# Two record tiles loaded apart, dropped nodes stored ahead of the other keys, merged loads and batch-norm statistics in a graph-layer kernel

## The chip, the core and the metric

The kernel runs on one core of a Trainium2 chip. The metric is the device time of one launch in microseconds (us), the median of several executions. The profile is one more execution, recorded by the hardware profiler. Engines: TensorE (PE), VectorE (DVE), ScalarE (ACT), GpSimd (POOL) and SyncE (SP). SP issues the plain transfers, POOL the indirect ones (gathers and scatters by a list of rows).

## What is computed

Sixteen batches of 1024 nodes with 64 channels, and for each batch a 1024 x 1024 adjacency with positive weights (about 4 neighbours in 1024 on average, but up to some 90 for the first nodes, whose probability is highest).

```python
# layer 0
h = maximum(layernorm(x), 0)
x = x + (adj / clip(sum(adj, 2), 1)) @ h
# layer 1
h = maximum(layernorm(x), 0)
nb   = (adj > 0) without the diagonal;  m = nb.sum(-1);  rank = cumsum(nb)
skip = (m + 1) // 2 where m > 10 (and the node is not masked)
removed = nb & (rank % skip == 0);  rem = removed | removed.T
valid = nb & ~rem, and the node itself
agg  = 0.25 * q25 + 0.5 * q50 + 0.25 * q75    # quantiles of h over the valid neighbours, per channel
x = x + (relu((h + agg) @ W1 + b1) @ W2 + b2) * mask
```

A node with more than ten neighbours drops two of them, and these must also drop it.

## The kernel before

`list_path` (lines 386 to 1485) does all the work; `dense_path` is a fallback behind a flag that stays zero with these inputs.

**A planner writes the order.** `Plan` (lines 246 to 345) runs when the program is built. Every stage is a Python generator that yields the engine of its next step and the earliest time it is thought to be ready; the planner emits, step by step, the stage that can begin first, and breaks ties by rank. The costs are those of `Plan.note` (a POOL indirect transfer takes 1.27 us and lands 2.2 us later, and so on). DVE and POOL keep exactly this order; the order of the others is settled by the framework's scheduler. Each engine executes its list in order, so an instruction that waits holds up all behind it, and a wrong guess of the planner becomes a wait.

**First stage, per batch** (`loads`, `beginnings`, `signs`, `listing`, `transposes`, `products`, `channels`, `endings`, lines 574 to 823). Eight tiles of 128 rows of the adjacency arrive, 512 KB each, in tiles named `at`. ACT takes signs (`sg`) with the row's sum; DVE multiplies them by position keys and takes the eight largest keys of each of four segments (`rec`): a record of up to 32 neighbours. PE transposes `at` (`pt`), ACT copies the result (`att`), PE multiplies (`ps_small`), DVE divides by the degree and adds x. `normed` (line 518) is the layer norm, called twice in each batch (for x, and for the sum): DVE sums, ACT squares with an accumulated sum in eight pairs of instructions (`ln_sq`), DVE and ACT make the root, ACT scales. The result and the record make up a row of 164 numbers (`row`). `endings` ranks the nodes by number of neighbours and scatters the rows, eight POOL calls in each batch, into a sorted table `srt`; the channels go to a table `tab`.

**Second stage, per group of four batches** (`group`, lines 1187 to 1322; four groups). When the 32 scatters of a group have landed, all 32 record tiles are loaded (`recs`, 544 KB, line 1202), the node numbers computed (`nodes_i`), and the adjacency rows of the 128 nodes with most neighbours gathered (`gat_rows`, line 1216). DVE counts and checks the lists (`gfound`, `gm`, `over`), searches the keys of 31 tiles (lines 1244 to 1253), removes dropped neighbours, and only then counts along the gathered rows (lines 1278 to 1291) which two columns each of these nodes drops. Two POOL calls store the dropped numbers in `tab` (`tab<-drop,didx`, lines 1293 to 1303). After these have landed, a `Job` for each of eleven list lengths gathers the neighbours' channels from `tab` (`places`, one POOL call for each neighbour place and tile, 124 in a group), sorts them by a network of DVE minima and maxima, weighs them, runs the two small layers and scatters the result (`out_dram`, 31 calls in a group). A job also loads its own channels (`S`, line 874) and its residual (`y`, line 1131), each with a transfer of its own.

**Third stage, the long lists** (`long_lists`, lines 1324 to 1458): the nodes with most neighbours of all batches, 128 at a time, in four lists of up to 88, 28, 21 and 18 neighbours. The order of adding the stages is:

```python
for g in range(NG - 1): plan.add(group(g), -2000)
...
with tc.tile_pool(name="long", bufs=1) as pool:
    plan.add(group(NG - 1, pool, "last_"), -2000)
    plan.add(long_lists(pool), -1500)
```

The last group and the long lists begin when the first stage has given back its memory.

Of the kernel before, what the change touches and what calls it, by code (L numbers as in the profile page):

```python
# [9 lines left out]
F32 = mybir.dt.float32  # L10
# [8 lines left out]
P = 128  # L19
# [366 lines left out]
def list_path(ctx, tc, x, adj, nodemask, w1, b1, w2, b2, out, go):  # L386
# [97 lines left out]

    before = consts.tile([P, NT], F32, name="before")
# [32 lines left out]
    def normed(h, xt):  # L518

        s = new(tiny, [P, NT], F32, "ln_s", 4)  # L520
        nc.vector.tensor_reduce(s, xt, AX.X, OP.add)
        nc.vector.tensor_scalar(s, s, -1.0 / C, None, op0=OP.mult)
        v = new(tiny, [P, NT], F32, "ln_v", 4)
        for t in range(NT):
            if t % 2 == 0:
                yield "ACT", lambda: at(s)
            sq = new(tiny, [P, C], F32, "ln_sq", 2)
            nc.scalar.activation(
                sq, xt[:, t, :], AF.Square, bias=s[:, t:t + 1], accum_out=v[:, t:t + 1]
            )  # L530
        yield "DVE", lambda: at(v) + SLACK
# [42 lines left out]
    def loads(pool, now):  # L574
        def nodes(st, b):
            yield "SP", lambda: room("xt", 3)
            st["xt"] = new(pool, [P, NT, C], F32, "xt", 3, users=1)
            nc.sync.dma_start(st["xt"], x[b].rearrange("(t p) c -> p t c", p=P))
            st["mrow"] = new(tiny, [NT, P], U8, "mrow", 3)
            nc.sync.dma_start(st["mrow"], nodemask[b].rearrange("(t p) -> t p", p=P))  # L580

        yield from nodes(batch[0], 0)
        for b, st in enumerate(batch):
            now[0] = b
            for t in range(NT):
                if t == 2 and b + 1 < B:
                    yield from nodes(batch[b + 1], b + 1)
                yield "SP", lambda: room("at", 5)
                st["rows"][t] = new(pool, [P, N], F32, "at", 5, users=2)
                nc.sync.dma_start(st["rows"][t], adj[b, t * P:(t + 1) * P, :])  # L590

    def beginnings(pool, now):

        for b, st in enumerate(batch):
            now[0] = b
            yield "DVE", lambda: max(known(st, "xt", "mrow"), room("h0", 3), room("row", 4))
            mrow_f = new(tiny, [NT, P], F32, "mrow_f", 2)
            nc.vector.tensor_copy(mrow_f, st["mrow"])

            h0 = new(pool, [P, NT, C + 1], F32, "h0", 3, users=2)  # L600
# [3 lines left out]
            yield from normed(h0[:, :, :C], st["xt"])  # L604
            st["h0"] = h0
            yield "PE", lambda: max(at(mrow_f), room("ps_small", 3))
            pm = new(ps_s, [P, HALF], F32, "ps_small", 3, users=1)
            nc.tensor.transpose(pm[:, :NT], mrow_f, ident[:NT, :NT])
            yield "ACT", lambda: at(pm)
            nc.scalar.copy(row[:, :, RW - 1], pm[:, :NT])  # L610
            nc.scalar.copy(row[:, :, RW - 2], row_f)
            free(pm)

    def signs(pool, now):
        for b, st in enumerate(batch):
            now[0] = b
            for t in range(NT):
                yield "ACT", lambda: max(
                    at(st["rows"][t]) if t in st["rows"] else INF, room("sg", 4),
# [4 lines left out]
                sg = new(pool, [P, N], HF, "sg", 4, users=1)  # L624
# [112 lines left out]
    def channels(pool, now):  # L737

        for b, st in enumerate(batch):
# [3 lines left out]
            yield from normed(row()[:, :, :C], row()[:, :, X1:R0])  # L743
# [100 lines left out]

    class Job:
# [3 lines left out]
        def __init__(self, pool, n, T, keys, idx, node, mask, nodes_i, table, S, g, name="places",  # L849
                     bufs=4, rank=0, half=False, begin=0.0):  # L850
# [6 lines left out]
        def run(self):  # L857
# [6 lines left out]
                self.begin, at(self.idx), room(self.name, self.bufs), room("S", 4) if short else 0.0  # L864
# [6 lines left out]
            if short:  # L871
                mine = self.S
                self.S = new(pool, [P, T, C], F32, "S", 4, users=1)
                nc.sync.dma_start(self.S, mine[:, :, :C])
                self.residual = mine[:, :, X1:R0]
# [248 lines left out]
        def layers(self, terms, sources):  # L1124

            T, R = self.T, terms[0][0].shape[1]
            yield "PE", lambda: max(at(*sources) + LOOSE, room("y", 6), room("pt", 2))
            y = new(mlp, [P, T, CO], F32, "y", 6, users=1)
            x1 = y
            if self.short:  # L1130
                nc.sync.dma_start(x1, self.residual)
            else:
                x1 = self.S[:, :, X1:R0]
# [52 lines left out]

    def group(g, kept=grp, name=""):

        size = GROUPS[g]
        four = size == 4  # L1190
        caps, caps_sb, s = (CAPS, caps4, 0) if four else (CAPS2, caps2, 2)
        NTAU = len(caps)
        begin = 1 if four else 0
        R = FIRST[g] + size

        yield "SP", lambda: 0.0 if progress["batches"] >= R and (
            g < 2 or name or progress["jobs"][g - 2] == len(set(CAPS[1:] if GROUPS[g - 2] == 4 else CAPS2))
        ) else INF
        table = tabs[g]
        recs = new(kept, [P, NTAU, REC], F32, name + "recs", 1 if name else 2)  # L1200
        tiles = srt[g].rearrange("(t p) w -> p t w", p=P)
        nc.sync.dma_start(recs, tiles[:, :, R0:])
        yield "DVE", lambda: at(recs)
        lists = recs[:, :, :8 * NSEG]
        node = recs[:, :, REC - 2]
        mask = recs[:, :, REC - 1]
        nodes = new(grp, [P, NTAU], F32, "nodes", 1)
        nc.vector.tensor_scalar(
            nodes, node, noff[:, s:s + 1], float(FIRST[g] * N), op0=OP.add, op1=OP.add
        )  # L1210
        nodes_i = new(kept, [P, NTAU], I32, name + "nodes_i", 1 if name else 2)
        nc.vector.tensor_copy(nodes_i, nodes)
        progress["begun"] = g + 1
        yield "POOL", lambda: at(nodes_i)
        full = new(grp, [P, N], F32, "gat_rows", 1)
        gather(full, adj_rows, nodes_i[:, 0:1])
        yield "DVE", always

        found = new(grp, [P, N], BF, "gfound", 1)[:, :NTAU * 8 * NSEG]
        found = found.rearrange("p (t e) -> p t e", t=NTAU)  # L1220
        nc.vector.tensor_scalar(found, lists, 0.0, None, op0=OP.is_gt)
        m = tiny.tile([P, NTAU], F32, name="gm")
        nc.vector.tensor_reduce(m, found, AX.X, OP.add)
        over = tiny.tile([P, NTAU], F32, name="over")
        nc.vector.tensor_reduce(
            over, found.rearrange("p t (s e) -> p t s e", e=8)[:, :, :, 7], AX.X, OP.max
        )
        nc.vector.memset(over[0 if four else HP:, 0:1], 0.0)
        big = tiny.tile([P, NTAU], F32, name="big")
        nc.vector.tensor_tensor(big, m, caps_sb, OP.is_gt)  # L1230
        nc.vector.tensor_tensor(over, over, big, OP.max)
        nc.vector.tensor_reduce(ovf[:, g:g + 1], over, AX.X, OP.max)

        base = toff[:, s:s + 1]
# [4 lines left out]

        drop = new(tiny, [P, 2, 2], F32, "drop", 2)  # L1240
# [3 lines left out]
        for t in range(begin, NTAU):  # L1244
            nc.vector.max(out=keys[:, t, :8], in_=lists[:, t, :])
            if caps[t] > 8:
                nc.vector.match_replace(
                    out=left, in_to_replace=keys[:, t, :8], in_values=lists[:, t, :],
                    imm_value=0.0,
                )  # L1250
                nc.vector.max(out=keys[:, t, 8:], in_=left)
            if t % 8 == 0:
                yield "DVE", always

        assert all(cap <= T_THRESH for cap in caps[begin + 1:])
        fst = slice(begin, begin + 1)
        skip = dilation(m[:, fst], mask[:, fst], 1)
# [6 lines left out]
        if four:  # L1264
# [504 lines left out]
```

## Time and profile before

| | |
|---|---|
| median of three executions | 1457.18 us (1456.25 to 1458.25) |
| the profiled execution | 1457.89 us |
| its span, first to last instruction | 1456.0 us |
| DVE busy | 1214.5 us |
| POOL busy | 960.6 us |
| PE busy | 745.0 us |
| ACT busy | 579.9 us |
| scatters of batches 0, 1, 2, 3 begin | 67.8, 100.6, 136.0, 168.6 us |
| first gather of `places` | 213.3 us |
| last scatter of batch 15 begins | 885.6 us |
| last gather of `places` ends | 1383 us |

How to read it. All recorded instructions carry line 240, that of a helper, so a group is known by its tiles: `places<-tab,idx` writes `places` from `tab` by the list `idx`. A view of waits says for which engine's instruction the engine sat idle, and for how long in all, how often, and at most. "issue" is idle time with no releaser in the profile: the gap between two POOL calls that follow one another is of this kind. A view of stages gives the busy time of each engine within a stretch of the span.

### The profile page before, as it was taken

The page shows a single profiled execution, that of the slowest core. Times are in us where ns is not written, and L with a number is a line of the kernel's source. Part 1 is how long each engine was busy: PE and PEld are TensorE (multiplying, and loading weights), DVE is VectorE, ACT ScalarE, POOL GpSimd, SP SyncE. Part 2 cuts the span into 40 slices and gives each one's busy share as a digit, 9 for nine tenths or more (in the row PEclk, how much of TensorE's full clock was granted, in tenths as well). Part 3 has the DMA queues.
Part 4 walks back from the last instruction along what each step waited for, and adds up shares of the span by engine and source line. Part 5 has one row for each costly group of instructions (what it writes and reads, how often), then busy time and mean ns, then how long its engine had stood idle before and what let it go on. Part 6 is the DMA issues. An engine that isn't in the chain of part 4 may idle for free.

```text
span 1456.0 us, 14752 instructions
## 1 busy us (share of the span) xinstructions
PE 745.0 (51%) x3186; PEld 463.6 (32%) x3186; DVE 1214.5 (83%) x4039; ACT 579.9 (40%) x1747; POOL 960.6 (66%) x1120
## 2 busy tenths in 40 slices
PE   4777877345697566783666660002300262134674
PEld 2434434223345434352443430001200141134453
DVE  6868798997989968899766874868999979999885
ACT  7989978444656527672353830000000010001110
POOL 0132227777767887677778576577777877777754
PEclk9879998668697687895587775555555575558576
DMA  5445567524464416472232334121111111212100
GB/s 183 138 128 184 176 199 203 137 52 143 100 175 117 107 34 181 121 191 78 71 108 76 87 70 89 42 55 44 37 23 24 27 29 27 41 34 46 24 16 14
DMA packets 134589, 132.20 MB, mean 91 GB/s; under 512 B 100196, under 2 KB 102884, under 8 KB 134372
## 3 DMA queue, kind: packets, MB, share of 16 engines
q1 hardware_dynamic: 102972, 91.00, 21.8%
q0 software_dynamic: 31520, 40.19, 12.8%
q8 instruction: 27, 0.44, 0.1%
q14 instruction: 70, 0.57, 0.1%
HBM read 111.62 MB, written 23.61 MB: 93 GB/s over the span
## 4 chain that ended last, share of the span: by engine, by line
DVE 36%; POOL 22%; issue 11%; PE 10%; DMA 10%; ACT 9%; SPq 0%; DVEq 0%; POOLq 0%; ACTq 0%
POOL places L240 14%; DVE places L240 6%; PE ps_small L240 5%; PE pt L240 5%; DMA at<-in_adj_dram 5%; DVE lplaces L240 4%; DVE other L240 4%; DVE rec L240 4%; DMA places<-tab,idx 3%; POOL out_dram L240 3%; ACT sg L240 3%; DVE l0other L240 3%; POOL lplaces L240 2%; ACT ln_sq L240 2%; DVE sg L240 2%
## 5 line engine op out<-in xcount | busy, mean ns | idle before, releaser
L240 POOL DMA_INDIRECT places<-tab,idx x372 | 375.5, 1009 | 114.5 <-issue 106.7
L240 PE MATMUL pt<-ident,prod 128*128 128x128 f32 (+1 forms) x736 | 162.0, 383 | 389.8 <-DVE prod L240 325.0
L240 PE MATMUL ps_small<-att,h 128*65 128x512 f32 x512 | 254.3, 644 | 27.9 <-ACT att L240 9.4
L240 PEld LDWEIGHTS pt<-ident,prod 128*128 128x128 f32 (+1 forms) x736 | 131.6, 264 | 422.2 <-issue 250.6
L240 POOL DMA_INDIRECT srt<-row,to x128 | 130.3, 1018 | 179.4 <-ACT row L240 158.6
L240 PE MATMUL pt<-ident,at 128*128 128x128 f32 x1024 | 168.4, 309 | 65.9 <-ACT att L240 51.8
L240 DVE MAX8 rec<-sg 128x8 f16<-128x256 f16 x512 | 180.1, 414 | 4.4
L240 POOL DMA_INDIRECT lplaces<-whole,lidx x125 | 145.4, 1164 | 38.1 <-issue 36.9
L240 ACT ACTIVATE sg<-at 128x1024 f16<-128x1024 f32 x128 | 134.9, 1054 | 87.0 <-DMA at<-in_adj_dram 75.1
L240 PEld LDWEIGHTS pt<-ident,at 128*128 128x128 f32 x1024 | 130.0, 158 | 113.8 <-ACT att L240 77.6
L240 POOL DMA_INDIRECT places<-tab,last_idx x124 | 133.5, 1077 | 37.8 <-issue 35.7
L240 ACT ACTIVATE wu<-wu 128x39 f32<-128x39 f32 (+9 forms) x40 | 9.4, 235 | 354.2 <-DVE wu L240 354.0
L240 ACT COPY att<-pt 128x512 f32<-128x512 f32 x256 | 142.0, 583 | 18.9 <-PE pt L240 16.9
L240 DVE TENSOR_TENSOR sg<-sg,keyed 128x1024 f16<-128x1024 f16 x128 | 87.3, 682 | 48.3 <-ACT sg L240 48.3
L240 PEld LDWEIGHTS ps_small<-att,h 128*65 128x65 f32 x512 | 73.8, 150 | 164.5 <-issue 122.7
L240 ACT COPY ot<-pt 128x128 f32<-128x128 f32 (+3 forms) x56 | 22.4, 400 | 220.5 <-PE pt L240 220.4
L240 POOL DMA_INDIRECT out_dram<-y,nodes_i x93 | 94.0, 1010 | 22.3 <-issue 13.3
L240 PE MATMUL ps_small<-ot,w_sb 128*128 128x128 f32 (+3 forms) x112 | 50.8, 544 | 29.5 <-ACT ot L240 16.0
L240 DVE TENSOR_TENSOR places<-places,other 128x128 f32<-128x128 f32 (+6 forms) x160 | 56.3, 354 | 3.3
L240 PE MATMUL ps_small<-w_sb,hid 128*128 128x64 f32 x256 | 51.8, 343 | 7.1 <-ACT hid L240 6.8
L240 ACT ACTIVATE hid<-ps_small,b_sb 128x128 f32<-128x128 f32 (+2 forms) x56 | 28.2, 504 | 64.0 <-PE ps_small L240 63.9
L240 DVE TENSOR_TENSOR places<-other,places 128x128 f32<-128x128 f32 (+5 forms) x136 | 48.7, 365 | 1.7
(270 smaller groups left out, 1635.3 us busy)
## 6 DMA issues: line engine op xcount, KB each, us to landing
at<-in_adj_dram SPq DMA_DIRECT2D x128, 512.0 KB
places<-tab,idx POOLq DMA_INDIRECT x372, 2.6
whole<-tab SPq DMA_DIRECT2D x4, 1057.0 KB
tab<-row SPq DMA_DIRECT2D x16, 264.0 KB
xt<-in_x_dram SPq DMA_DIRECT2D x16, 256.0 KB
srt<-row,to POOLq DMA_INDIRECT x128, 3.4
lplaces<-whole,lidx POOLq DMA_INDIRECT x125, 2.5
places<-tab,last_idx POOLq DMA_INDIRECT x124, 2.5
```

The source lines that it names most:

```text
L240: ins = getattr(self._engine, op)(*args, **kwargs)
```

## The change

- `recs0`: the first two record tiles are loaded by a small transfer of their own, ahead of the other 32 tiles. The nodes, the gather of `gat_rows`, the search of list 1, the count along the rows and the two stores into `tab` use only these. The search of the other 30 tiles, `idx` and all node numbers come after that.
- The overflow check of the lists (`gfound`, `gm`, `over`) becomes a stream of its own, of a low rank (`checked`).
- `at` is loaded in pairs of tiles, 1 MB each, in three buffers in place of five single ones; `sg` has three buffers in place of four, `h0` two in place of three.
- The node mask is loaded once, transposed once, and kept in `marks`; a batch copies two columns from it.
- `normed` takes a flag: in the first four batches DVE's `bn_stats` gives mean and variance, in place of DVE's sum and ACT's squares.
- In a group the five jobs with the longest lists (15, 10, 8, 7 and 6 neighbours, six tiles) share one `S` and one `y`, each loaded once.
- The rows of the four long lists are loaded by four transfers into one tile, in place of sixteen.

```diff
-    def normed(h, xt):
+    def normed(h, xt, stats=False):
         s = new(tiny, [P, NT], F32, "ln_s", 4)
-        ...
         v = new(tiny, [P, NT], F32, "ln_v", 4)
+        if stats:
+            st = new(tiny, [P, NT, 6], F32, "ln_st", 2)
+            for t in range(NT):
+                nc.vector.bn_stats(out=st[:, t, :], in_=xt[:, t, :])
+            apart = new(tiny, [P, NT], F32, "ln_apart", 2)
+            nc.vector.tensor_tensor(apart, st[:, :, 1], st[:, :, 4], OP.subtract)
+            nc.vector.tensor_tensor(s, st[:, :, 1], st[:, :, 4], OP.add)
+            nc.vector.tensor_tensor(v, st[:, :, 2], st[:, :, 5], OP.add)
+            nc.vector.scalar_tensor_tensor(
+                apart, apart, float(C) / 4.0, apart, op0=OP.mult, op1=OP.mult
+            )
+            nc.vector.tensor_tensor(v, v, apart, OP.add)
+            nc.vector.tensor_scalar(s, s, -0.5, None, op0=OP.mult)
+        else:
+            ...
     def loads(pool, now):
...
-                yield "SP", lambda: room("at", 5)
-                st["rows"][t] = new(pool, [P, N], F32, "at", 5, users=2)
-                nc.sync.dma_start(st["rows"][t], adj[b, t * P:(t + 1) * P, :])
+                if t % 2 == 0:
+                    yield "SP", lambda: room("at", 3)
+                    pair = new(pool, [P, 2, N], F32, "at", 3, users=4)
+                    nc.sync.dma_start(
+                        pair, adj[b, t * P:(t + 2) * P, :].rearrange("(k p) j -> p k j", p=P)
+                    )
+                st["rows"][t] = pair[:, t % 2, :]
...
-            yield from normed(h0[:, :, :C], st["xt"])
+            yield from normed(h0[:, :, :C], st["xt"], b < GROUPS[0])
...
-            yield from normed(row()[:, :, :C], row()[:, :, X1:R0])
+            yield from normed(row()[:, :, :C], row()[:, :, X1:R0], b < GROUPS[0])
     class Job:
...
+                if "S" not in share:
+                    S = share["S"] = new(
+                        pool, [P, mine_of(share), C], F32, "S", 4, users=share["users"]
+                    )
+                    nc.sync.dma_start(S, share["rows"][:, :, :C])
...
     def group(g, kept=grp, name=""):
...
+        recs0 = new(tiny, [P, 2, REC], F32, "recs0", 2)
+        nc.sync.dma_start(recs0, tiles[:, :2, R0:])
         recs = new(kept, [P, NTAU, REC], F32, name + "recs", 1 if name else 2)
         nc.sync.dma_start(recs, tiles[:, :, R0:])
-        yield "DVE", lambda: at(recs)
+        yield "DVE", lambda: at(recs0)
+        mine = recs0[:, 0, REC - 2:]
+        drop = new(tiny, [P, 2, 2], F32, "drop", 2)
+        full = yield from fetched(g, mine)
...
+        search(begin, recs0[:, 1, :8 * NSEG])
...
+        yield from counted(full, mine, drop)
+        yield "POOL", lambda: at(drop)
...
+        yield "DVE", lambda: at(recs)
+        for t in range(begin + 1, NTAU):
+            search(t, lists[:, t, :])
+        idx = new(kept, [P, NTAU, 16], I32, name + "idx", 1 if name else 2)
...
+        plan.add(checked(), 100 * g + 50)
     def long_lists(pool):
...
+        own_rows = new(pool, [P, len(LONG), RW], F32, "lS", 1)
+        for g in range(NG):
+            lo, num = FIRST[g] * LSUB, GROUPS[g] * LSUB
+            nc.sync.dma_start(
+                own_rows[lo:lo + num, :, :],
+                srt[g][:len(LONG) * num, :].rearrange("(l r) w -> r l w", l=len(LONG)),
+            )
```

`fetched` holds the node numbers of the first tile and the gather of `gat_rows`, `counted` the lines 1278 to 1291 of before; `search(t, mine)` is the body of the loop of lines 1244 to 1251. The planner then writes a new order for all engines.

## The prediction

> **What bounds the kernel now.** I read the busy times by slice first, for what is full where; then the stages of 40 us; then the waits of POOL and its timeline around each group's start.
>
> ```profile
> PE 745.0 (51%) x3186; PEld 463.6 (32%) x3186; DVE 1214.5 (83%) x4039; ACT 579.9 (40%) x1747; POOL 960.6 (66%) x1120
> DVE  6868798997989968899766874868999979999885
> ACT  7989978444656527672353830000000010001110
> POOL 0132227777767887677778576577777877777754
> ```
>
> A slice is 36.4 us. ACT leads in slices 1 to 5, POOL stands at seven or eight tenths from slice 7 to the end, DVE at nine tenths from slice 25. POOL at seven or eight is full: a call takes about 1.0 us and 0.3 us "issue" before it.
>
> ```profile
> 120.00:160.00 40.00, 30.75 (x134) 16.69 (x135) 32.62 (x104) 36.71 (x109) 8.96 (x16) 0.91 0.58 181
> 480.00:520.00 40.00, 23.66 (x73) 14.11 (x72) 37.72 (x135) 20.00 (x66) 31.35 (x39) 0.65 0.31 72
> 1080.00:1120.00 40.00, 0.00 (x0) 0.00 (x0) 39.48 (x113) 0.00 (x0) 31.46 (x29) 0.50 0.15 24
> ```
>
> Columns: PE, weight load, DVE, ACT, POOL. The three stages have different bounds: ACT at 92% (120 to 160), POOL full with DVE at 94% (480 to 520), DVE and POOL both full (1080 to 1120).
>
> ```profile
> POOL srt L240 <- ACT row L240: 158.6, 23, 63.7
> POOL gat_rows L240 <- DVE nodes_i L240: 23.9, 3, 12.6
> POOL tab L240 <- DVE deg L240: 17.3, 1, 17.3
> POOL gat_rows L240 <- DVE gfound L240: 16.1, 1, 16.1
> ```
>
> Most of the first line lies ahead of the first gather. The other three, 57.3 us, are group starts: 12.6, 7.4 and 3.9 us at the gathered rows of groups 0 to 2, 16.1 at those of the long lists, and this at group 0:
>
> ```profile
> 190.97 1.17 POOL L240 DMA_INDIRECT gat_rows<-in_adj_dram,nodes_i  x1 [12.55 <-DVE nodes_i L240]
> 209.48 0.98 POOL L240 DMA_INDIRECT tab<-drop,didx  x1 [17.34 <-DVE deg L240]
> ...
> 213.33 0.97 POOL L240 DMA_INDIRECT places<-tab,idx  x1 [1.41 <-DMA tab<-drop,didx]
> ```
>
> From 213 us POOL has 893 indirect calls in before's order and stops only at waits; what moves its waits moves the end.
>
> **What the skill says.** "DMA: Bandwidth & Descriptors", section "Anatomy of one DMA — SWDGE (gpsimd) path", prices a POOL transfer at a fixed 2.0 us plus bytes/436e3: the two stores into `tab` land 2.3 us after the second began (210.77 to its release at 213.1), which agrees. "VectorE: DVE Perf Modes", section "The TRN2 errata", gives 58 cycles plus elements at 0.96 GHz: 29 `MAX8` of 32 elements took 2.78 us, 96 ns each against 94; alone, a sum of 512 took 0.69 against 0.59, so some 150 fixed cycles where nothing overlaps. "Perfetto Trace Analysis", section "Optimization Strategy", says that the most contended engine can change between regimes; the three stages agree. No page I found prices `bn_stats` by name.
>
> **Part 1, statistics of batches 0 to 3.** A norm's sixteen `ln_sq` instructions take 2.64 us of ACT (chain, 16.07 to 18.71). Two norms: ACT loses 5.3 us a batch. The scatters begin at 67.8, 100.6, 136.0, 168.6, a period of 33.6 us, in which ACT is busy 30.3 and DVE 26.2 (35.39 + 36.71 and 29.83 + 32.62 in the 80 us from 80 to 160, scaled to 33.6). DVE adds eight `bn_stats` of 64 elements and six small operations for each norm. The trace has no `bn_stats`: lower bound (58+64)/0.96 = 0.127 us, upper (150+64)/0.96 = 0.223; I take 0.127, as the run of `MAX8` is so priced. Eight are 1.0 us, the small ones 1.0 more, less the sum and scaling that go (0.69 + 0.17): +1.2 a norm, +2.5 a batch (up to +4). ACT falls to 25.0, DVE rises to 28.7 (up to 30.2). So the busiest engine falls only from 30.3 to 28.7: three periods x 1.6 = -4.8. From batch 3's last products to its scatter (157.4 to 168.6 in the timeline) lies one norm; I take -5 for its squares and the root behind them. The first 1 MB pair lands later than the first tile did: +2.5 (0 if transfers overlap fully; 512 KB at 168 GB/s, about the 181 of 120 to 160, is +3.1). Sum -7; from -20 (the first term at ACT's pace, rival (a)) to +8 (DVE at its upper bound, and as the bound).
>
> **Part 2, the first two tiles apart.** `recs` is issued at 182.25, its reader runs at 190.24: 8.0 us for 544 KB. `recs0` is 34 KB; bounds 2.3 (the `tab` stores) and 8.0; I take 3. Then 0.5 (nodes, cast) and 0.3, a gather at 186.0; before, from its issue to the DVE multiplication that reads it went 190.97 to about 195.7, 4.7 us, to 190.75. Counting along the rows follows at once instead of after the other keys: 201.15 to 209.20 = 8.05, to 198.8. Store to first gather is 213.33 - 209.48 = 3.85, to 202.7. The other keys and `idx` (1.2 + 3.4 + 0.5 on DVE, behind the counting) end at 198.8 + 5.1 = 203.9 and are needed too: the first gather moves by -9.4. With part 1: 213.3 - 16.4 = 196.9.
>
> Later groups: in the order of POOL's calls before, the rows are calls 33, 185, 364, 533, the stores from 35, 201, 382, 550; after: 33, 206, 363, 526 and 35, 208, 374, 537. Between rows and stores stood 14, 16, 15 calls; now 0, 9, 9. So at group 1 POOL has nothing to do while the rows arrive and are counted: 4.7 + 8.05 + 0.3 = 13.0 us, against the 7.4 it waits today. At group 2 nine calls of 1.3 = 11.7 cover it but for 1 to 3 us (3.9 today). At the third change the long lists' gather no longer stands ahead of the stores: 2 us (16.1 today). SP: `recs0` adds four transfers of 34 KB ahead of `recs`; the queue there waits for scatters anyway.
>
> Place of the last scatter of batch 15: call 522 before, 521 after. Before: 213.3 + 487 x 1.32 + 32 of waits = 888, against 885.6 in the trace, so the average call of 1.32 holds. After: 196.9 + 486 x 1.32 + 27 (13 + 2 + 12 for other misjudged waits, the like of the 8.1 and 12.7 us at single scatters now) = 865, -20.
>
> At the third change DVE gets to the long lists' keys 34.6 us after that scatter against 38.8, as the check (0.69 + 1.22 + 0.37 + small ones, 3 us) comes later and the merged rows sooner: -4. The check itself is moved, not saved, and lies beside gathers in a stretch where DVE is 71% busy; without that cover it costs 3 x 3 us. POOL stores the dropped numbers 7 to 13 calls further up the list, and the 16-us wait goes: up to -9 on top of -20. From there to the end DVE's work is the same and it is 92 to 95% busy, so DVE's account is -20 - 4 + 3 (the deferred check) = -21, POOL's -29. What is late next is the sorting of the last gathers, which needs both; I take the middle, -25.
>
> **Part 3, transfers merged.** SP runs its list in order:
>
> ```profile
> SPq L240 <- DMA out_dram<-y,nodes_i: 405.8, 41, 96.0
> ```
>
> A `y` load waits for an old `y` to be scattered, and the `at` loads queue behind. Each group now needs 6 `y` tiles instead of 10 with the same six buffers; but the shared one is freed only when all five jobs have scattered. By the order it waits in group 1 for call 204 with 78 tiles issued (before: call 129, 69 tiles), later in much the same places. Costed at nothing; the cover is that POOL is full while `at` waits. If that cover goes, it is one DVE idle of the 12 us seen near 338, 544 and 792, in either direction. Long rows: sixteen transfers over 10.9 us become four; the gain is in the -4. The mask: sixteen loads and their transposes go, a few us of DMA and PE spread over 800 us, neither of which bounds: nothing.
>
> **Part 4, added waits.** Three `sg` in place of four: ACT waits for DVE's listing (0.69 + 1.41 = 2.1 us a tile), and the copies of `att` with PE behind wait with it. Lower bound nothing; upper one stall a tile. Two `h0`: DVE's write waits for PE's products, group work behind. Pairs of `at`: the next load waits for two tiles, SP's queue behind. ACT's sign today waits 11.5 us in all for `rec`, so four is just enough; I take 12 us for these, the 12 of part 2.
>
> **Sum.** Profiled execution 1457.89 = span 1456.0 + 1.9 outside; -25 gives 1432.9; it stood 0.7 above the median, so 1432.
>
> **Rivals.** (a) The first stage follows ACT: 33.6 x 25.0/30.3 = 27.7 a period, 3 x 5.9 = -17.7 instead of -4.8. For it: ACT is at 92%; against: DVE at 82% gets more work. 1432 - 12.9 = 1419.
> (b) The gain is swallowed: group 1's 13 us, and batches 4 to 7, which keep their old norm and arrive no sooner than `at` loads let them; DVE at 88% between 434 and 688 leaves little to catch up. -3: 1454.
> (c) Slower: the `sg` ring. If ACT stands for one listing step, 2.1 us, 1.5 times a batch in the 12 interleaved batches, that is +38, less the 25: 1470. It decides from about one stall a batch (12 x 2.1 = 25). For it: DVE runs group work between the listings, so a tile's key step can lie 2 us and more behind its sign; against: ACT is at 50% there, and the planner knows the ring.
> That the change does not do what it says is excluded by the new order, which has the stores moved and the squares gone.
>
> **Chances.** Forecast 0.60 (1420 to 1444), (a) 0.13, (b) 0.14, (c) 0.13. About 0.2% (2.9 us) is what a measurement can tell from no change. Faster: 0.60 + 0.13 + 0.08 of (b) = 0.81; same 0.06 from (b); slower 0.13. The range reaches from 9 under (a) to (b): 1410 to 1455; (c), and what of (a) and (b) lies beyond, are left out.
>
> **What would show it.** Right: scatters of batch 3 begin near 161 us and the first gather near 197; POOL waits some 13 us for the stores of group 1 and no 16 us at the long lists' rows; half the `ln_sq` instructions, `bn_stats` at 0.13 to 0.22 us; last scatter near 865, last gather near 1360. Wrong: ACT waiting for `rec` far above 11.5 us, SP's wait for `out_dram` above 406 with DVE idle, or DVE below 90% in the last stage, which would mean that POOL's waits and not DVE's work set the end.

## The result, and the profile after

The changed kernel took 1445.26 us (median of four, 1441.77 to 1448.27), the kernel before 1457.41 beside it: a ratio of 0.9916, interval 0.9891 to 0.9942, clear of 1. That is 12.2 us less, where 25 were forecast. The profiled execution took 1441.77 us (span 1440.0) and is the fastest of the four: the traces differ by 16.0 us, the medians by 12.2.

The page of the changed kernel, busy times and slices:

```profile
PE 739.0 (51%) x3171; PEld 463.6 (32%) x3171; DVE 1223.6 (85%) x4138; ACT 559.5 (39%) x1603; POOL 959.3 (67%) x1124
DVE  6988797999849899995998692989999699999895
ACT  6888774455644837753465332000000010001010
POOL 0042237777762788775788867777877777877854
```

There is a new hole in POOL's row, the 2 in slice 12 (counted from 0; 432 to 468 us), with a 4 in DVE's row in the slice before it. The same three stages (PE, weight load, DVE, ACT, POOL):

```profile
120.00:160.00 40.00, 33.11 (x128) 16.37 (x127) 33.72 (x126) 33.49 (x95) 8.79 (x16) 0.91 0.56 177
480.00:520.00 40.00, 22.86 (x119) 15.46 (x118) 37.53 (x121) 21.86 (x59) 32.24 (x42) 0.76 0.47 148
1080.00:1120.00 40.00, 0.00 (x0) 0.00 (x0) 39.54 (x131) 0.00 (x0) 31.11 (x30) 0.50 0.12 25
```

In the first stage ACT and DVE are now level, at 84%: neither is full. POOL's waits, the ones that matter:

```profile
POOL srt L240 <- ACT row L240: 137.9, 16, 65.3
POOL gat_rows L240 <- DMA at<-in_adj_dram: 16.6, 1, 16.6
POOL tab L240 <- DVE gfound L240: 13.9, 1, 13.9
POOL tab L240 <- DVE deg L240: 12.6, 1, 12.6
POOL gat_rows L240 <- DVE gbasep L240: 11.3, 1, 11.3
```

The 16.1 us at the long lists' rows are gone, and 16.6, 13.9 and 11.3 have come at groups 1 and 2. Two accounts show what this is worth. POOL's, where "waits" are the idle times over 0.45 us between the first and the last gather in its timeline, and "calls" all the rest of that stretch:

| us | before | changed | difference |
|---|---|---|---|
| first gather | 213.3 | 201.9 | -11.4 |
| waits | 51.0 | 52.7 | +1.7 |
| calls | 1118.9 | 1120.4 | +1.5 |
| last gather ends | 1383.2 | 1375.0 | -8.2 |
| from there to the end of the span | 72.8 | 65.0 | -7.8 |

And DVE's, whose busy and idle time make up the span: busy 1214.5 and 1223.6, +9.1; idle 241.6 and 216.4, -25.1. The idle time fell by 8.6 before the first gather, rose by 2.6 between that and the last scatter of batch 15, fell by 14.7 up to the last gather and by 4.4 after it. That scatter began at 888.2 us, 2.6 later than before, though the stage had begun 11.4 sooner.

So the middle stage, from the first gather to the last scatter, gave away all that the group start won. The largest new waits are at the start of group 1. POOL there before, at the rows and the first store, with 14 gathers in between:

```profile
415.05 1.17 POOL L240 DMA_INDIRECT gat_rows<-in_adj_dram,nodes_i  x1 [7.40 <-DVE nodes_i L240]
436.09 1.00 POOL L240 DMA_INDIRECT tab<-drop,didx  x1 [0.30 <-DVE other L240]
```

And in the changed kernel, from the last gather of group 0 to the first of group 1:

```profile
422.07 0.97 POOL L240 DMA_INDIRECT places<-tab,idx  x1 [0.30 <-issue]
439.59 0.96 POOL L240 DMA_INDIRECT gat_rows<-in_adj_dram,hnodes_i  x1 [16.55 <-DMA at<-in_adj_dram]
454.44 0.99 POOL L240 DMA_INDIRECT tab<-drop,didx  x1 [13.89 <-DVE gfound L240]
...
459.04 0.97 POOL L240 DMA_INDIRECT places<-tab,idx  x1 [2.31 <-DVE nodes L240]
```

SP and DVE at the same place:

```profile
399.19 0.37 SPq L240 DMA_DIRECT2D tab<-row  x1
418.09 0.88 SPq L240 DMA_DIRECT2D recs<-srt  x2
419.06 3.33 SPq L240 DMA_DIRECT2D at<-in_adj_dram  x2
```

```profile
428.09 0.69 DVE L240 TENSOR_TENSOR sg<-sg,keyed 128x1024 f16<-128x1024 f16 x1 [19.93 <-ACT sg L240]
...
438.94 0.20 DVE L240 TENSOR_SCALAR hnodes<-recs,noff 128x1 f32<-128x1 f32 x1
```

The scatters of batch 7 end at 416.7. Until then SP stands at the record loads, with two adjacency pairs behind them. DVE has no group work left and waits 19.9 us for the signs of the first pair, and the node numbers `hnodes` stand behind the listing of four tiles, two pairs. So the rows are asked for 22.9 us after the last scatter has ended, and then nothing is left to gather while they are fetched and counted: 16.55 + 13.89 + 2.31 = 32.8 us.

### The profile page after: what moved, and what is told of

It is laid out like the page before. It is cut to its first block, busy times and chain, and to the rows that moved or that the text cites. A ratio compares the mean times of both kernels' runs of the same rounds, so it can differ in the third digit from the quotient of the medians.

```text
span 1440.0 us, 14359 instructions
## 1 busy us (share of the span) xinstructions
PE 739.0 (51%) x3171; PEld 463.6 (32%) x3171; DVE 1223.6 (85%) x4138; ACT 559.5 (39%) x1603; POOL 959.3 (67%) x1124
## 4 chain that ended last, share of the span: by engine, by line
DVE 46%; POOL 18%; issue 11%; DMA 10%; PE 7%; ACT 6%; SPq 0%; DVEq 0%; POOLq 0%; ACTq 0%
POOL places L240 12%; DVE places L240 7%; DVE lplaces L240 6%; DVE rec L240 6%; DVE other L240 5%; DMA at<-in_adj_dram 5%; PE ps_small L240 4%; DVE l0other L240 4%; POOL lplaces L240 3%; PE pt L240 3%; DVE sg L240 2%; DMA places<-tab,idx 2%; DVE prod L240 2%; ACT sg L240 2%; DVE lother L240 1%
## 5 line engine op out<-in xcount | busy, mean ns | idle before, releaser
L240 POOL DMA_INDIRECT srt<-row,to x128 | 126.8, 990 | 160.2 <-ACT row L240 137.9
L240 PE MATMUL pt<-ident,at 128*128 128x128 f32 x1024 | 172.8, 316 | 95.1 <-ACT att L240 66.1
L240 PEld LDWEIGHTS pt<-ident,at 128*128 128x128 f32 x1024 | 134.0, 161 | 142.9 <-ACT att L240 93.8
L240 POOL DMA_INDIRECT lplaces<-whole,lidx x125 | 141.5, 1132 | 38.1 <-issue 36.6
L240 POOL DMA_INDIRECT places<-tab,last_idx x124 | 137.6, 1109 | 37.8 <-issue 35.4
L240 POOL DMA_INDIRECT out_dram<-y,nodes_i x93 | 96.0, 1032 | 21.0 <-issue 12.4
L240 ACT ACTIVATE row<-rec,before 128x32 f32<-128x32 f16 x128 | 39.1, 318 | 32.5 <-DVE rec L240 27.9
L240 DVE TENSOR_TENSOR other<-places 128x256 f32<-128x256 f32 (+4 forms) x124 | 48.4, 390 | 1.7
```

The lines of the kernel that those rows point to most:

```text
L240: ins = getattr(self._engine, op)(*args, **kwargs)
```

## The experiments

Theory: the order, not a resource, loses the time. With an earlier group start the planner puts more of group 0 ahead (scatters of batch 7 are POOL's calls 193 to 200, before 168 to 175), so group 1 starts with nothing to cover it, and the records block the adjacency loads on SP. (Scatters are numbered among POOL's indirect calls.) Rivals: smaller rings of tiles delay batches 4 to 7 whatever the order; `bn_stats` loads DVE; or the start of group 1 doesn't set the end.

Runs whose labels begin with the same letter were measured side by side, in one series. In series e, f, g and i the kernel before itself took 1818 to 1835 us, in series h 1457.36. Times are therefore compared by their ratio to the kernel before; the traces of g are set beside f1, of another series on the same chip. The ratios are as on record; the quotients of the medians differ from them by up to 0.8% (e3: 1812.5 to 1821.8 is 0.995).

| run | median us | ratio to the kernel before | interval |
|---|---|---|---|
| h1 records loaded by POOL | 1453.5 | 0.9969 | 0.9951 to 0.9987 |
| h2 planner cost 1.28 | 1439.1 | 0.9868 | 0.9843 to 0.9893 |
| h3 planner cost 1.26 | 1437.5 | 0.9859 | 0.9834 to 0.9884 |
| h4 records by POOL, two jobs held | 1438.6 | 0.9863 | 0.9837 to 0.9889 |
| f1 changed | 1820.9 | 0.9993 | 0.9964 to 1.0022 |
| e4, f2, i2 two jobs held | 1779.0, 1774.3, 1830.0 | 0.9748, 0.9740, 0.9990 | 0.9689 to 0.9806, 0.9663 to 0.9816, 0.9959 to 1.0022 |
| e2, f3 one load | 1787.6, 1796.5 | 0.9803, 0.9850 | 0.9748 to 0.9859, 0.9774 to 0.9926 |
| e1, f4, i1 old norm | 1823.1, 1825.4, 1849.1 | 1.0025, 1.0053, 1.0086 | 0.9993 to 1.0058, 1.0026 to 1.0080, 1.0052 to 1.0120 |
| e3 old group start | 1812.5 | 1.0018 | 0.9993 to 1.0043 |
| g2 old rings | 1804.7 | 0.9855 | 0.9831 to 0.9878 |
| g3 own S and y | 1786.3 | 0.9811 | 0.9726 to 0.9896 |
| g4 three jobs held | 1818.3 | 0.9906 | 0.9874 to 0.9938 |

**The two halves of the starved start.** h1 issues the record loads from POOL, right behind the scatters:

```diff
-        yield "SP", lambda: 0.0 if progress["batches"] >= R and (
+        yield "POOL", lambda: 0.0 if progress["batches"] >= R and (
...
-        nc.sync.dma_start(recs0, tiles[:, :2, R0:])
+        nc.gpsimd.dma_start(recs0, tiles[:, :2, R0:])
...
-        nc.sync.dma_start(recs, tiles[:, :, R0:])
+        nc.gpsimd.dma_start(recs, tiles[:, :, R0:])
```

> The changed kernel with the loads of the record tiles issued by POOL, right behind the scatters, so that no adjacency load stands behind them on SP. If the 16.6 us at the rows of group 1 come from SP's order (adjacency pair behind the records, the listing of that pair ahead of the node numbers on VectorE), that wait falls to 4 to 8 us and VectorE's wait for signs there to under 5 us; the 14 us of counting stay, since no call stands between rows and stores. The end moves by less than the wait, 0.985 to 0.995 of the kernel before where the changed kernel stands at 0.999, if the first stage of later batches sets the pace. Rival (the wait is there because group 0 is used up, whatever SP's order): still 15 us or more.

h4 does this and holds the last two jobs of groups 0 to 2 back as well (`HELD` is 2):

```diff
             yield "POOL", lambda: max(
                 self.begin, at(self.idx), room(self.name, self.bufs),
+                INF if progress["rows"] < self.hold else 0.0,
...
         full = yield from fetched(g, mine)
+        progress["rows"] = g + 1
...
+                hold=g + 2 if g < NG - 1 and i >= len(classes) - HELD else 0,
```

> The record loads on POOL and two jobs of groups 0 to 2 held back, both: nine calls stand between rows and stores of group 1. If both halves of the starved start are as said, POOL's waits around the rows of group 1 fall from 33 to under 10 us, and the time is at or below that of two jobs held alone, 0.965 to 0.975 of the kernel before. If what is won there is lost again before the last scatter, 0.974 to 0.990.

POOL at group 1 in h1, and then in h4:

```profile
435.64 2.52 POOL L240 DMA_DIRECT2D recs<-srt  x2 [2.80 <-DMA srt<-row,to]
439.75 1.02 POOL L240 DMA_INDIRECT gat_rows<-in_adj_dram,hnodes_i  x1 [1.60 <-DVE gbasep L240]
457.35 1.00 POOL L240 DMA_INDIRECT tab<-drop,didx  x1 [16.57 <-DVE gfound L240]
461.95 0.99 POOL L240 DMA_INDIRECT places<-tab,idx  x1 [2.30 <-DVE nodes L240]
```

```profile
423.24 2.53 POOL L241 DMA_DIRECT2D recs<-srt  x2 [4.19 <-issue]
429.19 1.03 POOL L241 DMA_INDIRECT gat_rows<-in_adj_dram,hnodes_i  x1 [3.42 <-DVE gbasep L241]
```

In h1 the 16.55 us ahead of the rows are 2.80 + 1.60, and DVE waits 9.7 us for the records there and not for signs: with the loads off SP that wait goes. The counting stays uncovered at 16.57. In h4 that goes too, as nine calls stand in between: 32.8 us are 7.6. Where these waits come from is shown by that. But h1 is slower than the changed kernel, outside the expected range, and h4 is at 0.9863, where 0.965 to 0.975 was expected if the wait counted, and 0.974 to 0.990 if its gain was lost before the last scatter. It was lost behind it: that scatter begins at 872.3 us, 15.9 sooner than in the changed kernel. POOL's waits between first and last gather are 42.4 and 41.4 instead of 52.7, but its busy time there is 901.6 and 902.1 instead of 888.5: six of the eight record loads fall into this stretch (2.5 us in each group, 7.5 in all) and cost POOL nothing while SP issued them; five and eight more scatters of `out_dram` fall into it too. In h1 the last scatter of batch 15 begins at 862.8 us, 25.4 sooner than in the changed kernel, and the end is 9.4 later: DVE's idle time is 33.9 less between first gather and last scatter, and after that scatter 95.3 us instead of 60.8. The middle stage's gain is there and is lost in the last stage; why, no run shows. So where the last scatter falls is no measure of the end.

**The order by itself.** One constant of the planner, nothing else:

```diff
-            time, after = (1.27, 2.2) if op == "indirect_dma_start" else (0.15, 0.1)
+            time, after = (1.28, 2.2) if op == "indirect_dma_start" else (0.15, 0.1)
```

> The changed kernel with the planner's cost of an indirect transfer at 1.28 instead of 1.27 us and nothing else changed: another order of the same work. If the order by itself is worth as much as the parts of the change, the time is off the changed kernel's by 0.5% or more in either direction; if the parts and not the order make the difference, within 0.3%.

> As the run before, with 1.26 us: a second order of the same work. Order theory: 0.5% or more off the changed kernel's time in either direction; parts theory: within 0.3%.

1439.1 and 1437.5 us, 6.2 and 7.7 under the changed kernel's median, which was measured apart (the kernel before stood at 1457.41 there and 1457.36 here): 0.43 and 0.53%, where the order theory asked for 0.5 or more. The interval of h3 is clear of the changed kernel's, that of h2 touches it; in the profiled executions the spans are 1440.0, 1438.2 and 1436.4, so the order is worth 2 to 8 us. POOL at the start of group 1 in h2:

```profile
441.65 0.97 POOL L240 DMA_INDIRECT gat_rows<-in_adj_dram,hnodes_i  x1 [18.10 <-DVE base L240]
457.34 0.98 POOL L240 DMA_INDIRECT tab<-drop,didx  x1 [14.72 <-DVE gfound L240]
```

It is starved in both runs: 18.10 + 14.72 + 2.35 = 35.2 us in h2, 17.81 + 13.85 + 2.35 = 34.0 in h3. Yet they end as soon as h4 with its 7.6 (1438.6). So the third rival stands: that the starved start sets the end is not shown, and the times of h1 and h4 (8 us above and 7 below the changed kernel's) are of the size that another order alone makes. In h2 the last gather even ends at 1390.7, 15.7 later than in the changed kernel, with POOL's waits at 62.3 us, and the end is 1.8 sooner: only 31.98 us of DVE's work lie behind that gather instead of 49.14. POOL's waits alone mislead. DVE's idle time is 216.4 us in the changed kernel, 216.1 in h2, 214.0 in h3, 218.2 in h4 and 224.8 in h1, with 1222 to 1225 busy. As the busy time hardly differs, this must follow the end: the account says where idle time lies, not what causes it.

**The cover alone, and the statistics alone, where the kernel before takes 1820 us.** The edit of h4 without that of h1, in three series:

> The changed kernel with the last two jobs of groups 0 to 2 (17 gathers) held back until the rows of the next group are fetched, so that POOL has calls while they are counted. Starved-start theory: POOL's idle around the rows of group 1 falls from 33 to about 17 us, batch 7's scatters begin about 20 us sooner than 406, and the time is 1430 to 1436. Rival (rings): batch 7 comes no sooner, the held gathers are then done later and nothing is won: 1443 to 1450.

> The changed kernel with the last two jobs of groups 0 to 2 (17 gathers) held back until the rows of the next group are fetched. Starved-start theory: POOL's idle around the rows of group 1 falls from 33 to about 17 us, and the time is 0.980 to 0.986 of the kernel before (1428 to 1437 us). Rival (the smaller rings of tiles delay batches 4 to 7 whatever the order): as the changed kernel or slower, 0.991 to 0.996.

> The changed kernel with two jobs of groups 0 to 2 held back, the record loads on SP. On a chip where the kernel before takes 1457 us: POOL's waits around the rows of group 1 fall from 33 to 12 to 18 us. If the cover of the start is what counts, the time is 0.982 to 0.987 of the kernel before (1431 to 1438 us); if VectorE's work sets the end whatever POOL waits for at group 1, it stays at 0.988 to 0.993.

In f1, the changed kernel itself, the starved start repeats to within 0.06 us, POOL at group 1 again:

> The changed kernel itself, so that it stands beside the others on one chip. Every theory expects what was measured: 0.9916 of the kernel before (0.9891 to 0.9942), 1445 us where the kernel before takes 1457; POOL stands some 33 us around the rows of group 1.

```profile
536.29 0.96 POOL L240 DMA_INDIRECT gat_rows<-in_adj_dram,hnodes_i  x1 [16.61 <-DVE base L240]
551.14 0.99 POOL L240 DMA_INDIRECT tab<-drop,didx  x1 [13.90 <-DVE gfound L240]
```

With two jobs held the first wait is 12.8, 12.1 and 12.4 us and the second is gone, as expected. In f2 the scatters of batch 7 begin 20.7 us sooner than in f1 beside it (481.8, 502.5), as this theory has it and not the one of the rings. The time does not repeat: 0.975, 0.974 and 0.999, for the same kernel. So an end time of these series can't carry a conclusion about a percent; of the waits at group 1 it is those at the stores, there or gone, that can.

> The changed kernel with the old norm (sum on VectorE, squares on ScalarE) in all batches; POOL's order of calls is the same as in the changed kernel. Starved-start theory (the second stage lost 14 us because group 0's gathers are used up when the scatters of batch 7 are made, so POOL stands 33 us at the start of group 1): the statistics are worth only what they moved the scatters of batch 3 by, so batch 3 scatters near 168 us, the first gather near 207, POOL still waits 30 us or more around the rows of group 1, and the time is 1449 to 1451, 5 more. Rival (the statistics overload VectorE, 0.206 us for each of 128 instructions where 0.127 was taken): no later, 1440 to 1446.

> The changed kernel with the old norm in all batches, the same order of POOL's calls. If the statistics are worth what they moved batch 3's scatters by, these begin near 168 instead of 163 us and the time is 0.994 to 0.996 of the kernel before (1448 to 1452 us). If the first stage of batches 4 to 7 sets the pace and not the start of group 0, nothing is lost: 0.990 to 0.993 (1443 to 1447 us).

> The changed kernel with the old norm in all batches; POOL's order is the same, so this is the one part that can be taken out without a new order. On a chip where the kernel before takes 1457 us: VectorE's busy time falls by 9 us (1223.5 to 1214.5), and its idle time grows by what the squares hold up. If the statistics were worth what the scatters of batch 3 moved by, 5.5 us, the time is 0.995 to 0.996 of the kernel before against 0.9916 for the changed kernel; if the lead is lost by batch 5's scatters, as on the slower chip (303.3 against 302.9 us), it is 0.990 to 0.993.

The edit leaves out the flag of `normed` in both places; POOL's order stays. In f4 the scatters of batch 3 begin 5.3 us later than in f1 (175.9, 170.6), those of batch 5 at 303.3 and 302.9, of batch 15 at 1144.7 and 1146.1 (the first of its eight); the profiled spans are 1820.7 and 1821.9. The lead is lost by batch 5 in the trace, yet the ratios (1.0053 and 0.9993) are apart, and all three of the old norm are above 1. What the statistics are worth stays open between nothing and 0.6%; where the kernel before takes 1457 us it was not measured. The three traces of this one kernel also show how far a wait can move with nothing changed: POOL stands 23.2, 16.3 and 23.7 us at the rows of group 1. (The expectation of e1 speaks of 0.206 us for each of 128 instructions; there are 64, and in a row they follow one another every 0.126 us, as the section on the prediction shows.)

**Single parts taken back.** All but one of these change POOL's order too, so that their times cannot be put down to their part.

> The changed kernel with the first two record tiles read from the one large load again; the counting still goes ahead of the other keys. By the order, batch 7's scatters are calls 172 to 179 instead of 193 to 200, and 10 calls stand between rows and stores of group 1 instead of none. Starved-start theory: the first gather comes 2 to 5 us later, but POOL's idle at group 1 falls from 33 to about 20 us: 1436 to 1442. Rival (the smaller rings of adjacency tiles, signs and h0 delay batches 4 to 7 whatever the order): 1447 to 1450, the delay of the load on top.

> The changed kernel with the first two record tiles read from the one large load again, the counting still ahead of the other keys; batch 7's scatters are then calls 172 to 179 of POOL instead of 193 to 200. Starved-start theory: the first gather comes up to 5 us later, but POOL's idle at group 1 falls from 33 to about 20 us: 0.983 to 0.990 of the kernel before (1433 to 1442 us). Rival (rings): 0.993 to 0.996, the delay of the load on top of the changed kernel.

`recs0` is made a part of the one load (`recs0 = recs[:, :2, :]`). POOL waits 21.5 and 21.4 us at group 1's rows and not at its stores, as expected; the first gather comes at 220.6 and 221.8 us, 12 to 13 later than in f1 (208.9) where 5 at most was expected. The time, 0.9803 and 0.9850, is in or below what the theory gave.

> The changed kernel with the group start as before: one load, all keys searched before the counting along the rows, stores after that; the check stays a stream of its own and all other parts stay. By the order, batch 7's scatters are calls 167 to 174 and 13 calls stand between rows and stores of group 1. Starved-start theory: the first gather is at 208 to 212, POOL's idle at group 1 about 10 us as in the kernel before, the last scatter of batch 15 near 878 instead of 888; part of the third stage's gain is kept: 1440 to 1448, about as the changed kernel. Rival (rings): the last scatter comes near 895 and the time is 1453 to 1460.

As e2, with `counted` and the stores moved behind the other keys. A miss: 31.1 + 8.0 us of waits at group 1 where 10 were expected, and the first gather at 217.1. The last scatter came 46 us sooner than in f1 of another series (1109.3, 1155.0) and the time was 1.0018: once more that scatter does not tell the end.

> The changed kernel with adjacency tiles loaded singly into five buffers, four buffers of signs and three of h0, as before. Rings theory: batches 4 to 7 are delayed by the smaller rings, so the scatters of batch 7 begin 15 to 20 us sooner than in the changed kernel and the time is 0.985 to 0.990 of the kernel before on a chip where the changed kernel stands at 0.999. Starved-start theory: batch 7's scatters are calls 191 to 198, 2 calls stand between rows and stores of group 1, so the idle there stays at 25 us or more and the time within 0.4% of the changed kernel's.

```diff
-                    yield "SP", lambda: room("at", 3)
+                yield "SP", lambda: room("at", 5)
...
-                    at(st["rows"][t]) if t in st["rows"] else INF, room("sg", 3),
+                    at(st["rows"][t]) if t in st["rows"] else INF, room("sg", 4),
...
-            yield "DVE", lambda: max(known(st, "xt"), room("h0", 2), room("row", 4))
+            yield "DVE", lambda: max(known(st, "xt"), room("h0", 3), room("row", 4))
```

Neither theory held: batch 7 came 9 us sooner than in f1 (493.4, 502.5), POOL's waits at group 1 were 4.2 + 10.2 + 2.5 = 16.9 us, the time 0.9855. Whether rings or order did it is open. In the first stage, where group work has not begun, the trace speaks for the rings: the scatters of batch 3 begin at 154.4 us, and at 163.0 to 170.6 in all the other 14 traces with the statistics; the period of the first four batches is 27.5 us instead of the changed kernel's 31.3.

> The changed kernel with own loads of S and y for each of the five jobs with the longest lists. Batch 7's scatters are then calls 185 to 192, and 8 calls stand between rows and stores of group 1. Starved-start theory: the idle at group 1 falls by 8 x 1.25 = 10 us and the time by 0.3 to 1% against the changed kernel. Rival (an own y load waits for scatters of out_dram with the adjacency loads behind it, as in the kernel before): 0.3 to 1% slower than the changed kernel.

The `shared` argument is left out. The waits at group 1 were 13.6 at the rows, none at the stores and 4.8 at the next gather, 14 us less than in f1 where 10 were expected, and the time 0.9811. Both favour the theory, but are no clean proof, for the reason above.

> The changed kernel with the last three jobs of groups 0 to 2 (35 gathers) held back until the rows of the next group are fetched; batch 7's scatters are calls 159 to 166. Starved-start theory, in which the held gathers only have to cover the 13 us of fetching and counting: no better than with two jobs held (0.974 of the kernel before), 0.972 to 0.980. Rival (it is not the cover of the start but the earlier place of the later batches' scatters that helps): better by as much again as two jobs gave, 0.945 to 0.955.

0.9906, where the theory had 0.972 to 0.980; 14.7 us of wait at the rows and none at the stores. Three held jobs are no better than two. The rival that later batches only have to be scattered sooner did not come true: batch 7 began at 465.5 us there, 37 sooner than in f1, and the time is far from 0.955.

> The kernel before, for its trace on a chip on which it takes some 1820 us (its own 1457 us were of another chip), so that the stages can be set against those of the changed kernel there. If the same things set the end as on the first chip: one wait of about 7 us at the rows of group 1, the scatters of batch 7 begin 20 us before those of the changed kernel (502), the last scatter comes within 5 us of the changed kernel's 1146, and its last stage is 15 to 20 us longer than the changed kernel's 676. If dispatch and not the order sets the pace there, the stages differ by less than 5 us each.

This is a single execution. First gather at 231.8 us, scatters of batch 7 from 468.4, last scatter 1167.4, end 1836.0, against 208.9, 502.5, 1155.0, 1821.9 in f1. Batch 7 did come sooner before, by 34 us. But instead of one wait of 7 us at group 1 there are 15.2 at the rows and 12.4 at the stores: in this trace the kernel before starves there too, so the two cannot show what the new order cost. The last stages are 669 and 667 us: the 18.6 us that the changed kernel won after the last scatter in the first two traces are not there.

## Why the prediction was wrong

The direction was right; the gain was twice too large against the medians (25 and 12.2), and 9 us too large against the traces (25 and 16.0). Those 9 us are the sum of misses of either sign: 5.0 up to the first gather, 17.6 from there to the last scatter, and 13.6 the other way behind it. By its steps:

**Part 1.** Forecast -7, measured -5.5 at the scatters of batch 3 (168.58 to 163.12). That these are close is luck. The three periods fell by 2.3 each (33.6 to 31.3), -7.0 where -4.8 was taken. The first pair and the last norm were to give +2.5 and -5; batch 0's scatters, which hold both, began 1.5 later. Its second norm, from DVE's first instruction to the first scatter, did fall from 13.8 to 9.1 us, but began 6.2 later, of which the later first sign (9.86 to 11.47) is 1.6. At batch 3 that norm gave 1.3 (11.14 to 9.85). The price of `bn_stats` was right. Eight in a row:

```profile
153.27 1.10 DVE L240 BATCH_NORM_STATS2 ln_st<-row 128x6 f32<-128x64 f32 x8
```

One alone lasts 0.206 us, but the next begins 0.126 us after it began, so that they overlap as the run of `MAX8` did; the 0.127 that I took from "VectorE: DVE Perf Modes", section "The TRN2 errata", agrees. DVE's +1.2 a norm was right too: 8 x 1.2 = 9.6, measured +9.1, and 8.4 between f4 and f1. What the sum lacks are the smaller rings, which I put at nothing in the first stage. From 65 to 160 us ACT waited 8.0 us for adjacency tiles and DVE 7.6 for signs; before it was 2.2 and 1.7, in g2 with the old rings 1.9 and nothing.

**Part 2, the first group.** Forecast -9.4 from the issue of the records to the first gather, measured 31.1 to 26.9, -4.1. The 8.0 us from issue to reader were no price of the load. In the profile of before DVE works without a break up to the reader, which stands behind a listing and a norm:

```profile
188.98 0.43 DVE L240 TENSOR_TENSOR row<-row,xt 128x256 f32<-128x256 f32 x1
189.44 0.69 DVE L240 TENSOR_REDUCE ln_s<-row 128x8 f32<-128x512 f32 x1
...
190.24 0.24 DVE L240 TENSOR_SCALAR nodes<-recs,noff 128x32 f32<-128x32 f32 x1
```

A smaller load alone could not win the 5 us. In the changed kernel DVE was again listing and ranking, until 181.3, 3.3 us past the 178 at which I had the node numbers; 1.2 more went to the sum of batch 4's products, between counting and the other keys. The counting was 8.06 us (8.05 taken). With 1.8 less between scatter and issue the first gather came at 201.9 instead of 196.9.

**Part 2, "27 of waits": the step that failed.** I counted 13.0 at group 1 for fetching and counting; that was 13.9. What I did not see was ahead of it: 16.55 us until the rows were asked for, and 2.3 behind. I had POOL's new places of the rows (206 for 185) and of the stores, and did not ask what had been put ahead of the scatters that they wait for: 25 calls of group 0. So neither POOL nor DVE had work when group 1's records landed, and SP's queue, costed at nothing in part 3 with the words "POOL is full while `at` waits", lost exactly that cover. I had named that risk, at one idle time of DVE of 12 us; it was 19.9. At group 2 the same, 11.3 + 0.8 where 1 to 3 were taken, with DVE waiting 12.6 us for signs. Against the 27 up to the last scatter stand 52.7; the average call with its gap was 1.30 us instead of 1.32, which gave 8 us back, so that this scatter came at 888.2 instead of 865.

**The premise under it.** "What moves its waits moves the end" did not hold either. h4 has 11.3 us less of POOL's waits than the changed kernel and a span 1.7 longer, h2 has 9.6 more and a span 1.8 shorter. So the 52.7 explain where the last scatter fell; what set the end in their place stays open.

**Part 2, the third change.** Forecast -5 (middle of -1 and -9) behind the last scatter, measured -18.6. POOL's own term was right: -9, measured 497.6 to 486.8 from that scatter to the last gather, -10.8. The remaining -7.8 lies behind the last gather, where I had nothing. The mis-sized term is DVE's, -1: its idle time behind that scatter fell from 79.9 to 60.8 us. That the lifted 16-us wait and the earlier stores made this gain is read from the trace; no run tested it alone.

**Parts 3 and 4.** SP's wait for `out_dram` fell from 405.8 to 198.5 us, and ACT's for `rec` rose from 11.5 to 44.6, some 33 us more where 12 were taken. Neither moved an end that could be told apart; for the first stage see part 1. The slower rival (c) needs ACT to be the bound in the middle stage; with 44.6 us of stalls and a faster kernel it did not happen.

**The rivals.** (a) gave 27.7 us a period for a first stage that follows ACT. The changed kernel has 31.3, g2 with the old rings 27.5: this pace was there to be had, as far as one run of another order can show it. (b), the gain swallowed at group 1, was the right mechanism for the middle stage, and more than swallowed: +14 us there. It gave 1454 because it had no gain behind the last scatter.

**Two readings** of the profile were off and enter no sum: 858 of POOL's indirect calls, not 893, lie behind 213 us (893 is the whole kernel), and DVE stands at nine tenths from slice 29, not 25.

## What to carry to other kernels

A step made earlier is worth something only if what it feeds was the last to arrive: list, from the new order, what stands ahead of each later start and what is left to cover it. The time from a load's issue to its reader is the load's price only where the reader's engine stands idle before it. Keep an account of busy and idle time by stage for the engine that ends the kernel: a stage that ends sooner may only have moved its idle time, as in h1, whose last scatter came 25 us sooner and whose end 9 us later. Where a planner writes the order, change a constant that means nothing by a hundredth first: here that alone gave 2 to 8 us, where all the parts under study together gave 12.

## What was not expected of the hardware

In the series with 1818 to 1835 us single instructions lasted as long as elsewhere (DVE busy 1224.9 us in f1 and 1223.6 in the first trace of this kernel, POOL's calls 1.32 and 1.35 us with their issue), but engines stood idle with no releaser on the core, and POOL's waits were 438.6 us instead of 52.7. The same short chain of DVE in the first trace, and then in f1:

```profile
289.53 0.38 DVE L240 TENSOR_SCALAR d<-d 128x8 f32<-128x8 f32 x1
289.95 1.17 DVE L240 SCALAR_TENSOR_TENSOR d<-total,d 128x8 f32<-128x8 f32 x6
```

```profile
348.64 0.17 DVE L240 SCALAR_TENSOR_TENSOR d<-total,d 128x8 f32<-128x8 f32 x1 [1.22 <-issue]
350.04 0.17 DVE L240 SCALAR_TENSOR_TENSOR d<-total,d 128x8 f32<-128x8 f32 x1 [1.23 <-issue]
```

Six such operations took 1.17 us there; here each is 0.17 and 0.55 to 1.9 us apart. Up to the scatters of batch 1 the two traces agree (97.8 and 97.9 us); between 98 and 205 us ACT has two such gaps (2.9 and 2.8 us), and of its 500 us of them in f1 nearly all lie behind the first gather. The granted TensorE clock between 200 and 800 us was 0.68 in f1 and 0.76 in the first trace (0.91 and 0.88 up to 100 us); which follows from which is not shown. One and the same chip was in both conditions, in f and g and then in h. The cause stays open.
